# MLP input of a two-layer graph kernel: attention's output stored as two 16-bit planes, transposed by the DMA and joined on ScalarE

## The chip, the cores and the metric

The kernel runs on one core of one Trainium2 chip. The metric is the device time of one execution in microseconds (us). Three runs of the kernel before took 2292.01 us in the median (2291.98 to 2293.26).

## The reference, cut to what matters

3327 nodes with 1024 features pass through two layers, each added to its input. Layer 0 multiplies a dense adjacency matrix by a quantised product. Layer 1 is a graph attention with 8 heads of width 64, followed by an MLP of four dense layers:

```python
Wh = jnp.einsum('nf,hfd->hnd', x, W)
e = jax.nn.leaky_relu(e_src[:, :, None] + e_dst[:, None, :], ALPHA)
e = jnp.where(adj[None] > 0, e, NEG)
att = jax.nn.softmax(e, axis=-1)
h = jax.nn.elu(jnp.einsum('hnm,hmd->hnd', att, Wh))
enc = jnp.transpose(h, (1, 0, 2)).reshape(x.shape[0], -1)   # 3327 x 512
out = jax.nn.relu(enc @ W1.T + b1)     # 512 -> 256
out = jax.nn.relu(out @ W2.T + b2)     # 256 -> 256
out = jax.nn.relu(out @ W3.T + b3)     # 256 -> 512
out = out @ W4.T + b4                  # 512 -> 1024, added to x
```

All values are float32. The change concerns the way of `enc` from attention into the first of these dense layers.

## The kernel before, in words

The nodes are cut into 26 tiles of 128 rows. Layer 0 and the head projections fill the first part of the span. Attention runs as 32 passes (list `attends`), each for one head and one of four sets of 6 or 7 node tiles. A pass walks over 26 source tiles `j`. VectorE builds the selection `sel` (L729), TensorE multiplies it into up to seven accumulators (L738), and between these the generator `all_edges` feeds TensorE with a second product (L539), whose operand `mf` ScalarE casts from the mask (L538) and whose result `part` ScalarE copies out of PSUM (L543).

At the end of a pass ScalarE copies the accumulators to `xs` (L753), and the generator `close` finishes the pass a few instructions at a time while the next pass runs: VectorE sums and a reciprocal (L580 to L590), scaling on ScalarE (L593), the two activations of the ELU (L595, L596), the last step of the ELU on VectorE (L600), and one DMA from GpSimd's queue (L604), which stores a 64-column strip of 6 or 7 tiles into the DRAM tensor `enc_d`, 26 x 128 rows of 512 float32.

The MLP works on groups of four tiles (512 columns), seven groups with the last of two tiles. `load_nodes` (L664) loads a group's rows of `enc_d` (L667) and of the residual `x1_d` (L669) from SyncE's queue into one of two buffers, `nodes0` and `nodes1`, each of which holds an `enc` part and an `x1` part. The dense layers need features on partitions, so TensorE transposes `enc` in blocks of 128x128 against an identity matrix into PSUM (L797, name `tp`), ScalarE copies the four resulting blocks into `enct` (L800), and the function `dense` (L766) does a layer: matmuls (L772) and a ReLU with bias on ScalarE (L779). The last layer is kept with nodes on partitions (L809). VectorE adds the bias to `x1` (L805), then adds the product (L819), and SyncE's queue stores the result (L821). The first group's transposes and first dense layer are done during the last attention pass by the generator `first_layer` (L681: transposes L686, copies L691, matmuls L696, ReLU L704); its input sits in `nodes0`, and its `enct0` and `h1_0` in the tile `rest`.

The order of each engine's instructions is fixed before the run. A scheduler replays the program with estimated durations and puts each instruction into its engine's queue when its inputs and buffers are ready; earlier lines of the program go first where two are ready. On the chip each queue is then worked off in that order, and an instruction whose inputs are late holds up all behind it. Calls of `pin` fix VectorE's order in attention to the order of the program. Nothing in the MLP is pinned.

Buffers: `s3` holds the tiles of `close` (`ht3` with two buffers, the others one); the pool `s4` of the MLP has two buffers of each of `enct`, `h1`, `h2`, `h3`, `yo`; PSUM has four banks for `ps`/`tp4` and two double banks for the last product `o`.

Of the kernel before, what the change touches and what calls it, by code (L numbers as in the profile page):

```python
# [8 lines left out]
F32 = mybir.dt.float32  # L9
BF16 = mybir.dt.bfloat16  # L10
F32R = mybir.dt.float32r
U8 = mybir.dt.uint8
I8 = mybir.dt.int8
AF = mybir.ActivationFunctionType
ALU = mybir.AluOpType
# [4 lines left out]
P = 128  # L20
N = 3327
T = (N + P - 1) // P
NP = T * P
# [5 lines left out]
HD = 64  # L29
EMB = NH * HD  # L30
# [29 lines left out]
def two_layer_kernel(  # L60
# [23 lines left out]
    nc = tc.nc  # L84
# [15 lines left out]
    feat_d = dram.tile([T, NH, P, HW], F32, name="feat_d")  # L100
    dsum_d = dram.tile([T, NPAIR, P, HW], F32, name="dsum_d")
    src_d = [dram.tile([NH, len(sub) * P], F32, name=f"src_d{i}") for i, sub in enumerate(SUBS)]
    enc_d = dram.tile([NP, EMB], F32, name="enc_d")

    const.tile([P, 120], F32, name="gap")
    ndst = const.tile([P, T, NH], F32, name="ndst")
# [47 lines left out]
    def normaliser(mv, n, eps, factor, tag):  # L154

        rs = inverse_std(mv[:, :, 1], n, eps, tag)
        nc.vector.tensor_scalar(rs, rs, factor, None, ALU.mult)
        nb = small.tile([P, n], F32, tag=f"{tag}n", name=f"{tag}n")
        nc.vector.scalar_tensor_tensor(nb, mv[:, :, 0], -1.0, rs, ALU.mult, ALU.mult)
        return rs, nb  # L160

# [322 lines left out]
    with tc.tile_pool(name="f1", bufs=1, reuse_waits="tile") as f1p, tc.tile_pool(  # L486
# [81 lines left out]
        def close(i):  # L568


            c, g, e, si = attends[i]
            h = 2 * g + e
            sub = halves[c][si]
            nb = len(sub)
            md = mds[i // 4][:, sub[0] - 13 * c : sub[0] - 13 * c + nb, e * HC : (e + 1) * HC]
            sums = EDGE * (i // 4) + (EDGE if si else 7 * T)
            yield 0
            su = s3.tile([P, 7, 2, HC], F32, tag="su", name="su")
            s2d = su.rearrange("p b q c -> p b (q c)")
            pin(nc.vector.tensor_tensor(s2d[:, :nb], xs[:, :nb, 0], xs[:, :nb, 1], ALU.add))  # L580
            up, dn = su[:, :nb, 0], su[:, :nb, 1]
            for b, t in enumerate(sub):
                nc.scalar.activation(up[:, b], up[:, b], AF.Copy, scale=ratio[:, t, h : h + 1])  # L583
            yield sums
            pin(nc.vector.tensor_tensor(dn, md, dn, ALU.subtract))
            yield 0
            pin(nc.vector.tensor_tensor(up, up, dn, ALU.add))
            yield 0
            rs = small.tile([P, 7, 1], F32, tag="rs", name="rs")
            pin(nc.vector.reciprocal(rs[:, :nb], up[:, :, HD:]))  # L590
            ht = s3.tile([P, 7, HD], F32, tag="ht3", name="ht3", bufs=2)
            for b in range(nb):
                nc.scalar.activation(ht[:, b], up[:, b, :HD], AF.Copy, scale=rs[:, b])  # L593
            ex = s3.tile([P, 7, HD], F32, tag="ex", name="ex")
            nc.scalar.activation(ex[:, :nb], ht[:, :nb], AF.Relu, scale=-1.0)  # L595
            nc.scalar.activation(ex[:, :nb], ex[:, :nb], AF.Exp, scale=-1.0)  # L596
            yield 0

            pin(
                nc.vector.scalar_tensor_tensor(  # L600
                    ht[:, :nb], ex[:, :nb], -1.0, ht[:, :nb], ALU.add, ALU.max
                )
            )
            nc.gpsimd.dma_start(  # L604
                enc_d[sub[0] * P : (sub[-1] + 1) * P, h * HD : (h + 1) * HD].rearrange(
                    "(b p) d -> p b d", p=P
                ),
                ht[:, :nb],
            )

        def pin(ins):
            tc.keep_in_program_order(ins)
# [21 lines left out]
        for i, (c, g, e, si) in enumerate(attends):  # L634
            if i == len(attends) - 1:

                early.close()
                mlp = ctx.enter_context(ExitStack())

                def nodes(name):  # L640
                    n = large(mlp, name, [P, T * HW])
                    return (
                        n[:, : 4 * EMB].rearrange("p (q e) -> p q e", q=4),
                        n[:, 4 * EMB : 4 * (EMB + F)].rearrange("p (q e) -> p q e", q=4),
                    )

                weights = large(mlp, "weights", [P, T * HW])
                enc_x1 = [nodes("nodes0")]
                rest = large(mlp, "rest", [P, 7 * NP // 4])
                bb4 = rest[:, :F]  # L650
                bb1, bb2, bb3 = (rest[:, F + 4 * q : F + 4 * q + 4] for q in range(3))
                h1_0 = rest[:, F + 16 : F + 16 + D1 // P * 512].rearrange("p (m c) -> p m c", c=512)
                enct0 = rest[:, 2 * F + 16 : 2 * F + 16 + EMB // P * 512].rearrange(
                    "p (k c) -> p k c", c=512
                )
                w_at = iter((0, EMB * D1 // P, (EMB * D1 + D1 * D2) // P, (EMB * D1 + D1 * D2 + D2 * D3) // P))

                def weight(ap, k, m):
                    at = next(w_at)
                    wt = weights[:, at : at + k * m].rearrange("p (k m) -> p k m", k=k)  # L660
                    nc.sync.dma_start(wt, ap.rearrange("(k p) m -> p k m", p=P))
                    return wt

                def load_nodes(i, t0):  # L664
                    enc, x1 = enc_x1[i]
                    for q, t in enumerate(range(t0, min(t0 + 4, T))):
                        nc.sync.dma_start(enc[:, q, :], enc_d[t * P : (t + 1) * P, :])  # L667
                    for q, t in enumerate(range(t0, min(t0 + 4, T))):
                        nc.sync.dma_start(x1[:, q, :], x1_d[t * P : (t + 1) * P, :])  # L669

                load_nodes(0, 0)
                w1 = weight(w1t, EMB // P, D1)
                with nc.allow_non_contiguous_dma(reason="biases of a few hundred elements"):
                    for bb, ap in ((bb1, b1), (bb2, b2), (bb3, b3)):
                        m = ap.shape[0] // P
                        nc.sync.dma_start(bb[:, :m], ap.rearrange("(m p) -> p m", p=P))
                w2, w3 = weight(w2t, D1 // P, D2), weight(w3t, D2 // P, D3)
                w4 = weight(w4t, D3 // P, F)
                nc.sync.dma_start(bb4, b4.partition_broadcast(P))

                def first_layer():  # L681

                    for k in range(EMB // P):
                        tp = m_ps.tile([P, 512], F32, tag="mps", name="tp0")
                        for q in range(4):
                            nc.tensor.transpose(  # L686
                                tp[:, q * P : (q + 1) * P],
                                enc_x1[0][0][:, q, k * P : (k + 1) * P],
                                ident,
                            )  # L690
                        nc.scalar.copy(enct0[:, k], tp)  # L691
                        yield
                    for m in range(D1 // P):
                        ps = m_ps.tile([P, 512], F32, tag="mps", name="h0_ps")
                        for k in range(EMB // P):
                            nc.tensor.matmul(  # L696
                                ps,
                                w1[:, k, m * P : (m + 1) * P],
                                enct0[:, k],
                                start=(k == 0),  # L700
                                stop=(k == EMB // P - 1),
                            )
                            if k == EMB // P - 1:
                                nc.scalar.activation(  # L704
                                    h1_0[:, m], ps, AF.Relu, bias=bb1[:, m : m + 1]
                                )
                            yield

                first_group = first_layer()
            h = 2 * g + e  # L710
# [49 lines left out]
    with tc.tile_pool(name="s4", bufs=2, reuse_waits="tile") as s4, tc.tile_pool(  # L760
# [23 lines left out]
        for g, t0 in enumerate(range(0, T, 4)):  # L784
            tiles = range(t0, min(t0 + 4, T))
            cols = len(tiles) * P
            enc, x1 = enc_x1[g % 2]
            if t0 + 4 < T:
                load_nodes((g + 1) % 2, t0 + 4)
            if g == 0:  # L790
                h1 = h1_0
            else:
                enct = s4.tile([P, EMB // P, 512], F32, name="enct")
                for k in range(EMB // P):
                    tp = ps_p.tile([P, 512], F32, tag="ps", name="tp4")
                    for q, t in enumerate(tiles):
                        nc.tensor.transpose(  # L797
                            tp[:, q * P : (q + 1) * P], enc[:, q, k * P : (k + 1) * P], ident
                        )
                    nc.scalar.copy(enct[:, k, :cols], tp[:, :cols])  # L800
                h1 = dense(enct, EMB // P, w1, bb1, D1 // P, cols, "h1")
            h2 = dense(h1, D1 // P, w2, bb2, D2 // P, cols, "h2")
            h3 = dense(h2, D2 // P, w3, bb3, D3 // P, cols, "h3")
# [61 lines left out]
```

## Time and profile before

| | |
|---|---|
| median of 3 runs | 2292.01 us |
| the profiled execution | 2293.44 us |
| its span, first to last instruction | 2291.7 us |
| TensorE busy | 2233.5 us, 97% |
| VectorE busy | 1559.1 us, 68% |
| ScalarE busy | 998.2 us, 44% |
| GpSimd busy | 119.3 us, 5% |
| mean granted TensorE clock | 0.995 |
| MLP after attention's last matmul | about 1989.8 to 2287 us of the span |

A matmul's record can overlap that of its neighbours, so a busy TensorE is read from what it gets through in a stretch rather than from its share. In the rows, "idle before" is the time that the engine stood idle just ahead of these instructions, followed by what ended it. Weight loads of TensorE have rows of their own (PEld). SPq and POOLq rows are DMA issues of SyncE and GpSimd.

### The profile page before, as it was taken

Reading aid. Unit: us, or ns where it says so; the run is one execution under the profiler, and the core shown is the slowest. Engines: PE = TensorE matmul, PEld = TensorE weight load, DVE = VectorE, ACT = ScalarE, POOL = GpSimd, SP = SyncE. Lnnn points to the kernel's source line nnn. Section 1 sums busy time; section 2 is a strip of 40 time slices with the busy share of each in tenths; the row PEclk is TensorE's granted clock in tenths of the full one; section 3 lists DMA queues with packets and bytes.
Section 4 is the critical chain, followed back from the end, with each engine's and each line's share of the span. In section 5 each row is a group of like instructions: output and inputs, shape, how many; then the busy total and the mean of one; then the engine's idle time right before and its main releaser. Section 6 shows DMA issues by size and latency. Waiting matters only on the chain. (4 is left out here: it accounts for less than half of the span.)

```text
span 2291.7 us, 32041 instructions
## 1 busy us (share of the span) xinstructions
PE 2233.5 (97%) x12896; PEld 1785.0 (78%) x12896; DVE 1559.1 (68%) x2090; ACT 998.2 (44%) x1654; POOL 119.3 (5%) x173
## 2 busy tenths in 40 slices
PE   4999999999999999889999999999999999999999
PEld 2467777777777777579999999999999999744444
DVE  7845555555555555487999999999999999732211
ACT  4753333333333333346555555555555555411120
POOL 0000110111101111000000000000000000000000
PEclk9999999999999999999999999999999999999999
DMA  6324444444445444763324142654242422343311
GB/s 234 129 82 149 151 150 142 162 145 155 151 141 162 151 149 152 239 210 118 99 73 134 45 142 80 215 178 154 84 144 77 141 87 75 112 152 123 125 55 55
DMA packets 150301, 304.94 MB, mean 133 GB/s; under 512 B 10172, under 2 KB 91020, under 8 KB 150152
## 3 DMA queue, kind: packets, MB, share of 16 engines
q1 hardware_dynamic: 130248, 229.72, 30.3%
q0 software_dynamic: 19904, 73.17, 9.9%
q8 instruction: 101, 1.65, 0.3%
q14 instruction: 48, 0.39, 0.1%
HBM read 216.07 MB, written 86.79 MB: 132 GB/s over the span
## 5 line engine op out<-in xcount | busy, mean ns | idle before, releaser
L729 DVE SCALAR_TENSOR_TENSOR sel<-srow,ndst,mask 128x896 fp32r<-128x896 f32 (+1 forms) x832 | 864.1, 1079 | 54.4 <-PE acc L738 41.2
L539 PE MATMUL mps<-dw,mf 128*128 128x260 f32 x2704 | 453.3, 283 | 0.1
L444 PE MATMUL mm<-s_int,hi 128*128 128x512 f32 x1352 | 433.0, 399 | 0.0
L444 PE MATMUL mm<-s_int,lo 128*128 128x512 f32 x1352 | 421.6, 391 | 0.0
L738 PE MATMUL acc<-f_even,sel 128*128 128x260 f32 x2704 | 396.9, 284 | 1.4 <-DVE sel L729 1.1
L738 PE MATMUL acc<-f_odd,sel 128*128 128x260 f32 x2704 | 395.0, 286 | 0.0
L538 ACT CAST mf<-mask 128x1664 fp32r<-128x1664 uint8 x208 | 331.3, 1593 | 123.5 <-PE mps L539 100.2
L539 PEld LDWEIGHTS mps<-dw,mf 128*128 128x128 f32 x2704 | 377.7, 188 | 0.3 <-ACT part L543 0.3
L738 PEld LDWEIGHTS acc<-f_odd,sel 128*128 128x128 f32 x2704 | 353.4, 188 | 7.3 <-issue 3.1
L738 PEld LDWEIGHTS acc<-f_even,sel 128*128 128x128 f32 x2704 | 354.9, 188 | 5.4 <-DVE sel L729 2.8
L444 PEld LDWEIGHTS mm<-s_int,lo 128*128 128x128 f32 x1352 | 253.8, 188 | 57.6 <-issue 5.7
L444 PEld LDWEIGHTS mm<-s_int,hi 128*128 128x128 f32 x1352 | 252.1, 188 | 55.6 <-issue 5.7
L184 DVE TENSOR_SCALAR mk<-at 128x896 uint8<-128x896 f32 x104 | 61.7, 594 | 267.1 <-DMA at<-in_adj_t 266.1
L179 ACT CAST hi<-at 128x896 fp32r<-128x896 f32 x104 | 92.7, 891 | 328.8 <-PE mm L444 294.8
L385 PE MATMUL whm<-whead,ht 128*128 128x512 f32 x416 | 186.7, 602 | 0.8 <-ACT ht L382 0.8
L809 PE MATMUL o<-weights,h 128*128 128x512 f32 x416 | 179.7, 592 | 0.0
L809 PEld LDWEIGHTS o<-weights,h 128*128 128x128 f32 x416 | 79.0, 190 | 99.1 <-issue 99.0
L385 PEld LDWEIGHTS whm<-whead,ht 128*128 128x128 f32 x416 | 77.4, 191 | 98.0 <-issue 87.8
L183 DVE TENSOR_TENSOR lo<-at,hi 128x896 fp32r<-128x896 f32 x104 | 106.6, 1025 | 49.0 <-ACT hi L179 38.8
L543 ACT COPY part<-mps 128x260 f32<-128x260 f32 x104 | 39.3, 378 | 223.9 <-PE mps L539 223.9
L819 DVE TENSOR_TENSOR yo<-o,nodes 128x1024 f32<-128x1024 f32 (+1 forms) x27 | 31.8, 1182 | 139.2 <-PE o L809 139.2
L333 PE MATMUL mm<-w_int,xqt 128*128 128x512 bf16 x416 | 97.7, 386 | 10.2 <-DVE w_int L319 7.7
(136 smaller groups left out, 1567.8 us busy)
## 6 DMA issues: line engine op xcount, KB each, us to landing
feat_d<-fw POOLq DMA_DIRECT2D x26, 1040.0 KB, 5.3
f_even<-feat_d SPq DMA_DIRECT2D x7, 3380.0 KB, 13.1
f_odd<-feat_d SPq DMA_DIRECT2D x7, 3380.0 KB, 12.3
at<-in_adj_t SPq DMA_DIRECT2D x52, 448.0 KB, 4.2
at<-in_adj_t SPq DMA_DIRECT2D x52, 384.0 KB, 3.2
mask<-mask_d SPq DMA_DIRECT2D x39, 416.0 KB, 6.9
dw<-dsum_d SPq DMA_DIRECT2D x16, 910.0 KB, 8.9
dsum_d<-dw POOLq DMA_DIRECT2D x26, 520.0 KB, 6.5
```

The source lines that it names most:

```text
L179: ins = nc.scalar.copy(hi, at)
L183: nc.vector.tensor_tensor(lo, at, hi.bitcast(F32), ALU.subtract)
L184: nc.vector.tensor_scalar(mk[:, r], at, 0.0, None, ALU.is_gt)
L333: nc.tensor.matmul(mm[:, c * 512 : (c + 1) * 512], xqts[t][:, k, :], w_int[:, k, c * 512 : (c + 1) * 512], start=(k == 0), stop=(k == KF - 1),
L385: nc.tensor.matmul(whm, ht[:, k, :], whead[:, k, :], start=(k == 0), stop=(k == KF - 1))
L444: nc.tensor.matmul(mm[:, c * 512 : (c + 1) * 512], which[:, q, :], s_int[j][:, c * 512 : (c + 1) * 512], start=(j == 0 and which is hi), s ...
L538: nc.scalar.copy(mf, mask[:, j : j + TH, :])
L539: nc.tensor.matmul(ps, mf[:, j % TH, :], dw[:, j, :], start=(j == 0), stop=(j == T - 1))
L543: nc.scalar.copy(part[:, i % 7], ps.rearrange("p (q c) -> p q c", q=2))
L729: nc.vector.scalar_tensor_tensor(sel[:, :nb], srow[:, :nb], ndst[:, j, h : h + 1], mask[:, :, j, :], ALU.is_gt, ALU.mult,)
L738: nc.tensor.matmul(accs[b], sel[:, b, :], f[:, j, :], start=(j == 0), stop=(j == T - 1))
L809: nc.tensor.matmul(ps[:, c * 512 : (c + 1) * 512], h3[:, k, q * P : (q + 1) * P], w4[:, k, c * 512 : (c + 1) * 512], start=(k == 0), stop= ...
```

## The change

`enc_d` becomes a tensor of two planes of 16-bit integers: the low and the high halves of each float32. At the end of `close` a ScalarE copy (tile `eh`, one buffer) splits the words of `ht` into the two halves, and GpSimd issues two DMAs, one for each plane, in place of one. `load_nodes` reads a group's rows with two transposing DMAs (one for each plane, issued from SyncE's queue) in place of up to four plain ones; features then lie on partitions. A ScalarE copy for each of the four blocks of 128 features interleaves the two halves again into float32. TensorE's transposes and the copies out of PSUM are gone. For the first group the joining copies take the place of the transposes in `first_layer`; for the others they are written in the program one group ahead, right after the loads of the next group.

```diff
-    enc_d = dram.tile([NP, EMB], F32, name="enc_d")
+    enc_d = dram.tile([2, NP, EMB], U16, name="enc_d")
...
+    def halves_of_words(words):
+
+        return words.bitcast(U16).rearrange("p (n two) -> p two n", two=2)
...
-            nc.gpsimd.dma_start(
-                enc_d[sub[0] * P : (sub[-1] + 1) * P, h * HD : (h + 1) * HD].rearrange(
-                    "(b p) d -> p b d", p=P
-                ),
-                ht[:, :nb],
-            )
+            eh = s3.tile([P, 2, 7 * HD], U16, tag="eh", name="eh")[:, :, : nb * HD]
+            nc.scalar.copy(eh, halves_of_words(ht[:, :nb].rearrange("p b d -> p (b d)")))
+            for q in range(2):
+                nc.gpsimd.dma_start(
+                    enc_d[q, sub[0] * P : (sub[-1] + 1) * P, h * HD : (h + 1) * HD].rearrange(
+                        "(b p) d -> p b d", p=P
+                    ),
+                    eh[:, q].rearrange("p (b d) -> p b d", d=HD),
+                )
...
-                        n[:, : 4 * EMB].rearrange("p (q e) -> p q e", q=4),
+                        n[:, : 4 * EMB].bitcast(U16).rearrange("p (q r) -> p q r", q=2),
...
+                def by_feature(enc, cols):
+
+                    k = EMB // P
+                    return enc[:, :, : k * cols].rearrange("p q (k c) -> p q k c", k=k)
+
                 def load_nodes(i, t0):
                     enc, x1 = enc_x1[i]
-                    for q, t in enumerate(range(t0, min(t0 + 4, T))):
-                        nc.sync.dma_start(enc[:, q, :], enc_d[t * P : (t + 1) * P, :])
+                    rows = slice(t0 * P, min(t0 + 4, T) * P)
+                    for q in range(2):
+                        nc.sync.dma_start_transpose(by_feature(enc, rows.stop - rows.start)[:, q], enc_d[q, rows])
...
                     for k in range(EMB // P):
-                        tp = m_ps.tile([P, 512], F32, tag="mps", name="tp0")
-                        for q in range(4):
-                            nc.tensor.transpose(
-                                tp[:, q * P : (q + 1) * P],
-                                enc_x1[0][0][:, q, k * P : (k + 1) * P],
-                                ident,
-                            )
-                        nc.scalar.copy(enct0[:, k], tp)
+                        nc.scalar.copy(
+                            halves_of_words(enct0[:, k]), by_feature(enc_x1[0][0], 512)[:, :, k]
+                        )
                         yield
...
-            enc, x1 = enc_x1[g % 2]
+            x1 = enc_x1[g % 2][1]
+            enct = following if g else None
             if t0 + 4 < T:
                 load_nodes((g + 1) % 2, t0 + 4)
+                following = s4.tile([P, EMB // P, 512], F32, name="enct")
+                n = (min(t0 + 8, T) - t0 - 4) * P
+                for k in range(EMB // P):
+                    nc.scalar.copy(
+                        halves_of_words(following[:, k, :n]),
+                        by_feature(enc_x1[(g + 1) % 2][0], n)[:, :, k],
+                    )
             if g == 0:
                 h1 = h1_0
             else:
-                enct = s4.tile([P, EMB // P, 512], F32, name="enct")
-                for k in range(EMB // P):
-                    tp = ps_p.tile([P, 512], F32, tag="ps", name="tp4")
-                    for q, t in enumerate(tiles):
-                        nc.tensor.transpose(
-                            tp[:, q * P : (q + 1) * P], enc[:, q, k * P : (k + 1) * P], ident
-                        )
-                    nc.scalar.copy(enct[:, k, :cols], tp[:, :cols])
                 h1 = dense(enct, EMB // P, w1, bb1, D1 // P, cols, "h1")
```

More of the change, by code (lines that the diff above doesn't have):

```diff
@@ L12 @@
 U8 = mybir.dt.uint8
+U16 = mybir.dt.uint16
 I8 = mybir.dt.int8
```

## The prediction

> **What bounds the kernel now.** I read the page's busy times first, then the chain that ended last in order of time, because the change is in one stage. From 1992 us on, the chain is nearly all TensorE. One full group of four tiles:
>
> ```profile
> PE 2233.5 (97%) x12896; PEld 1785.0 (78%) x12896; DVE 1559.1 (68%) x2090; ACT 998.2 (44%) x1654; POOL 119.3 (5%) x173
> ...
> 2028.68 1.75 PE tp L797 x16
> 2030.42 17.54 PE h_ps L772 x40
> 2047.97 27.47 PE o L809 x64
> 2075.43 1.75 PE tp L797 x16
> ...
> 2262.46 0.87 PE tp L797 x8
> ```
>
> A group is 1.75 + 17.54 + 27.47 = 46.76 us of TensorE, end to end, and nothing stands between. So what the transposes take in this chain is really on the path: five full groups (1 to 5) and the half group 6.
>
> Next, the groups by shape from 1960 us on, the copies that the change removes, and, from the whole span, the one ScalarE copy of as many 16-bit elements as the new ones:
>
> ```profile
> L797 PE MATMUL tp<-ident,nodes 128*128 128x128 f32 x88 | 10.6, 273 | 0.0
> L800 ACT COPY enct<-tp 128x512 f32<-128x512 f32 x20 | 10.3, 600 | 136.2 <-PE tp L797 136.2
> ...
> L284 ACT COPY xqt<-tp 128x1024 bf16<-128x1024 bf16 x26 | 26.1, 1005 | 2.0 <-PE tp L282 1.9
> ```
>
> ScalarE idles 136 us here waiting for TensorE, so it has room. Where this room lies I read from its timeline in group 1:
>
> ```profile
> 2037.33 0.69 ACT L779 ACTIVATE h<-h_ps,rest 128x512 f32<-128x512 f32 x1 [2.75 <-PE h_ps L772]
> 2039.23 0.69 ACT L779 ACTIVATE h<-h_ps,rest 128x512 f32<-128x512 f32 x1 [1.22 <-PE h_ps L772]
> 2040.95 0.69 ACT L779 ACTIVATE h<-h_ps,rest 128x512 f32<-128x512 f32 x1 [1.03 <-PE h_ps L772]
> ```
>
> After the last ReLU of a group, at 2048.7 us, it does nothing until 2075.9. SyncE's queue shows when loads go out:
>
> ```profile
> 1969.47 1.78 SPq L667 DMA_DIRECT2D nodes<-enc_d  x4
> ...
> 2001.41 1.75 SPq L667 DMA_DIRECT2D nodes<-enc_d  x4
> 2003.20 2.03 SPq L669 DMA_DIRECT2D nodes<-x_d  x4
> 2011.26 0.34 SPq L821 DMA_DIRECT2D out<-yo  x1
> ...
> 2031.49 2.00 SPq L667 DMA_DIRECT2D nodes<-enc_d  x3
> 2056.12 0.34 SPq L821 DMA_DIRECT2D out<-yo  x1
> ```
>
> The loads at 1969.47 are those of group 2: they go out as soon as `nodes0` has been read (SyncE waited 8.9 us for the transposes L686), some 105 us before group 2 begins. The scheduler thus hoists loads about two groups ahead.
>
> **What the Trainium skill says.** "Advanced Engine Details and Errata", X-Bar Transpose (TRN2): transposing DMAs are as fast as regular ones, 350 to 400 GB/s expected. "DMA: Bandwidth & Descriptors", Latency and other measured facts: 261 GB/s on one kernel. "VectorE: DVE Perf Modes", The three transpose paths: 1309 ns for one 128x128 bf16 block. The trace before has no transposing DMA, so none of these is confirmed. "ScalarE: Activation LUTs", What ACT_TABLE_LOAD costs: an ACTIVATE with immediate operands takes 186 ns + 0.833 ns an element, which is 1039 ns for 1024; the trace agrees (1005 ns, row L284).
>
> **The change part by part.**
>
> *Removed from the MLP:* 5 x 1.75 + 0.87 = 9.6 us of TensorE on the path. The 24 copies L800 (11.5 us) go too, but ScalarE wasn't the bound.
>
> *Removed from the last pass of attention:* 16 transposes, about 16 x 0.109 = 1.75 us of TensorE. VectorE is busy 48.8 of the 50 us from 1940 to 1990 and paces this pass (TensorE's weight loads wait for `sel` at 1963, 1966 and 1970 us), so a lighter TensorE mostly waits longer. Between 0 and 1.75 us; I take 0.
>
> *Transposing DMAs:* 14 in place of 26 loads, two for each group, 1.05 MB a pair. At 261 to 400 GB/s a pair is 2.6 to 4 us of transfer (an estimate from the two pages), at 32 blocks x 1309 ns it is 42 us. The nearest row, four plain loads of 256 KB, lands about 4 us after its last issue. I take 5 to 10 us to landing, since the pieces are short. The cover: a buffer's `enc` part is free once the joining copies of the group in it are done, about 13 us into the group before last, and is wanted a whole group later. On the queue the pair stands behind the last `x1` load (2030.97) and ahead of the next store (2056.12). From 13 us into the group that leaves some 13 us free, and the two banks of `o` and two buffers of `yo` forgive about 6 us more: with a tile each 6.87 us and L819 at 1.22 us, VectorE may be 5.6 us late. Cost 0 up to some 19 us a pair; what lies above is paid in each group.
>
> *Joining copies:* 28 in place of 28 copies, but of 1024 16-bit elements: 1.0 us each for 0.6, 4.0 us a group. They may start when the `enct` buffer of the group before last is free, after a group's last h1 matmul (2037.3), so likely between the ReLUs above, in gaps of 1.22 and 1.03 us, or after them in 27 us of idle time. One ReLU is sensitive, the last of h2 (2040.95), since the second half of h3's first product waits for it: at most 0.1 us late with a copy of 1.0 us, 1 us with one twice as long. I take 0.1 us x 5 groups = 0.5 us; bounds 0 and 5.
>
> *Change of stage (1989 to 2015 us):* ScalarE is busy 8.1 of 11 us from 1990 on, and TensorE already waits for two ReLUs (0.57 and some 1.5 us). The copies of group 2 can fall here, as its loads are in long before: four copies of 1 us in a queue with 3 us of room. I take 1 us; bounds 0 and 4. Group 1's loads wait for the last store of attention. That store now follows a ScalarE copy (0.8 us) and a second issue (0.9 us), so the pair goes out near 2004.3 instead of 2001.4, and the `x1` loads queue behind it. VectorE stood idle 10.8 us for the first of these (until 2008.87), with L819 of the first tile behind it in its queue. TensorE needs this bank back at 2014.8. A delay of 3 + 4 us puts L819's end at 2018 unless the new order has it ahead of that L805. I take 1 us; bounds 0 and 6.
>
> *Splitting copies:* 16 of 896 and 16 of 768 elements. The casts of as many float32 elements (L179) take 945 and 837 ns, so 16 x 0.945 + 16 x 0.837 = 28.5 us of ScalarE over some 930 us of attention. Each waits for VectorE (L600); behind it on ScalarE stand the mask casts `mf` and the copies `part`, for which TensorE waits. The cover is the idle time of ScalarE:
>
> ```profile
> L538 ACT CAST mf<-mask 128x1664 fp32r<-128x1664 uint8 x208 | 331.3, 1593 | 123.5 <-PE mps L539 100.2 <-issue 21.6 <-ACT su L583 1.1
> L593 ACT ACTIVATE ht<-su,rs 128x64 f32<-128x64 f32 x208 | 53.5, 337 | 66.7 <-DVE rs L590 36.2 <-issue 30.0 <-ACT h L779 0.3
> L543 ACT COPY part<-mps 128x260 f32<-128x260 f32 x104 | 39.3, 378 | 223.9 <-PE mps L539 223.9
> L539 PE MATMUL mps<-dw,mf 128*128 128x260 f32 x2704 | 453.3, 283 | 0.1
> ```
>
> ScalarE already stands at L593 for VectorE, 66.7 us in all, and TensorE's L539 lost 0.1 us. One more such wait has the 223.9 us ahead of `part` to lie in. I take 0.5 us; bounds 0 and 28.5, all uncovered. The 32 added issues of GpSimd are 32 x 0.91 = 29 us on an engine that is 5% busy, and hidden. The stores' pieces shrink from 256 to 128 bytes at unchanged bytes, while the DMA is about a third busy in attention: hidden.
>
> *Sum:* -9.6 + 0.5 + 1 + 1 + 0.5 = -6.6 us. Against the profiled execution (2293.44, of which 2291.7 are span) that is 2286.8; that execution was 1.4 us above the median, so on the median's footing 2292.0 - 6.6 = 2285.4.
>
> **The rivals.**
>
> *A wash (chance 0.2).* The savings stand, but the change of stage and attention take 5 to 10 us: the bounds of 4 and 6 us both met, or a fifth of the splitting copies uncovered. For it: `mps` has one PSUM bank, so a late `part` stops L539 at once. Against: no stall of L539 before. 2292.0 - 9.6 + 10 = 2292.4, range 2287.5 to 2296.5.
>
> *Slow crossbar (0.17), the one on the other side.* The pair takes longer than the 19 us that the queue forgives, and stores, `x1` loads and the joining copies are late in each group. It decides from 19 us a pair. At 25 us: 5 groups x 6 us - 9.6 = +20, 2312; at 42 us: 5 x 23 - 9.6 = +105, 2397. For it: the 1309 ns. Against: the two bandwidths, which put the pair at 4 us.
>
> *Order on ScalarE (0.15).* The copies of the next group stand in ScalarE's queue ahead of the ReLUs of the current one, and these wait for the transposes or for four copies in a row: 4 us less the 1 to 2 us of slack in a group, or more where a transfer is late. From 1.75 us a group it eats the gain. At 3 us over 6 groups: +18 - 9.6 = +8, 2300. For it: the copies come first in the program. Against: loads two groups ahead.
>
> **How the numbers follow.** The forecast (2281 to 2287.5 as its own range: 1.75 us of attention's transposes gained and no losses, against twice the losses) has 0.48. 0.2% is 4.6 us, about what a measurement here can tell from no change. Faster 0.48; within 0.2%, the wash, 0.2; slower 0.32, from the last two. From the forecast's low end of 2281 up to 2310 the range leaves out most of the slow crossbar and little else, about 0.18.
>
> **What would show it.** Right: a chain of h_ps and o alone, 45.0 us a group; no TensorE transposes from 1960 us on; transposing DMAs landing within 10 us; joining copies near 1.0 us whose idle time ends on TensorE or DMA without a ReLU behind. L539's idle time stays below 1 us. Wrong: waits of L819 or L805 for DMA, of h_ps for ReLUs over 1 us a group, or a later end of attention than 1989 us. My weakest number is the crossbar's time, for which no row stands.

## The result, and the profile after

The changed kernel takes 2282.07 us in the median (2281.76 to 2283.57, 4 runs) against 2292.11 us of four runs of the kernel before, timed beside it: -10.0 us, ratio 0.9956 with a 95% interval of 0.9939 to 0.9974. The time lies inside the predicted range, below the predicted 2285.4; the direction was as forecast, the size was 10.0 where 6.6 was said. The profiled execution has a span of 2281.8 us against 2291.7, 9.9 us less, so the two profiles can be set against each other.

The chain that ended last, of the kernel after (its longer pieces: start in us, length in us, what): a group of the MLP with joining copies among its ReLUs, the first of three such, and then one without.

```profile
2000.07 27.47 PE o L818 x64
2027.54 6.88 PE h_ps L781 x16
2035.03 2.53 ACT enct L803 x2
2038.15 7.19 PE h_ps L781 x16
2045.34 27.47 PE o L818 x64
...
2163.31 17.56 PE h_ps L781 x40
2180.87 27.47 PE o L818 x64
```

The 1.75 us of transposes ahead of each group are gone. Groups 1, 2 and 3 take 45.27, 45.25 and 45.25 us (from 2027.54 to 2072.81, 2118.06 and 2163.31), groups 4 and 5 take 45.02 and 45.01; all took 46.76 before. In the first three, two joining copies have come into the chain, which was TensorE's alone.

The groups of instructions of the kernel after, over the whole span (busy time, mean ns of one, idle time before and its cause): TensorE's second product of attention, the copy behind it, and the new splitting copies.

```profile
L544 PE MATMUL mps<-dw,mf 128*128 128x260 f32 x2704 | 453.6, 283 | 0.1
L548 ACT COPY part<-mps 128x260 f32<-128x260 f32 x104 | 39.2, 377 | 194.4 <-PE mps L544 194.4
L610 ACT COPY eh<-ht 128x896 uint16<-128x896 uint16 (+1 forms) x32 | 28.3, 884 | 7.0 <-DVE ht L605 7.0
```

The same view by shape, from 1945 us on:

```profile
L803 ACT COPY enct<-nodes 128x1024 uint16<-128x1024 uint16 x20 | 25.3, 1333 | 9.4 <-DMA nodes<-enc_d 9.4
```

The 28.3 us of splitting copies stand in the shadow of `part`: its idle time went from 223.9 to 194.4 us, and TensorE's L544 lost the same 0.1 us as before. The joining copies take 1333 ns, not the 1.0 us of the prediction.

SyncE's queue of the kernel after: the transposing DMAs, of group 0, group 2, group 1 and then group 3.

```profile
1927.91 4.98 SPq L681 DMA_TRANSPOSE nodes<-enc_d  x2
1963.40 11.53 SPq L681 DMA_TRANSPOSE nodes<-enc_d  x2
2003.31 4.74 SPq L681 DMA_TRANSPOSE nodes<-enc_d  x2
2008.11 2.00 SPq L683 DMA_DIRECT2D nodes<-x_d  x4
2015.14 4.93 SPq L681 DMA_TRANSPOSE nodes<-enc_d  x1
```

A pair occupies SyncE for about 5 us, since each issue takes about 2.5 us; a single one lands 5.0 us after its issue (median). The pair at 1963.40 took 11.5 us, while the weights of the MLP were being loaded. The loads are hoisted as before, group 2's even ahead of group 1's.

Stage by stage, from the starts in the two traces: up to the loads of group 0 the kernel after is 0.36 us earlier (1927.91 for 1928.27), although the splitting copies and their stores came on top; across the kernels below this mark lies between 1926.8 and 1929.5, so 0.36 us can't be told from their spread. From there to h2's first matmul of group 0 it takes 60.75 us (to 1988.66) where 61.53 (to 1989.80) were needed: -0.78. From there to the first matmul after group 0 both take 38.88 us: 0. From there to the end 254.26 us for 263.02: -8.76. Together -9.9 us.

### The profile page after: what moved, and what is told of

It reads as the page before. It is cut to its first block, busy times and chain, and to the rows that moved or that the text cites. A ratio compares the mean times of both kernels' runs of the same rounds, so it can differ in the third digit from the quotient of the medians.

```text
span 2281.8 us, 31860 instructions
## 1 busy us (share of the span) xinstructions
PE 2222.5 (97%) x12780; PEld 1774.4 (78%) x12792; DVE 1559.8 (68%) x2090; ACT 1040.8 (46%) x1686; POOL 147.7 (6%) x205
## 4 chain that ended last, share of the span: by engine, by line
PE 52%; ACT 1%; DVE 0%; DMA 0%; issue 0%; SPq 0%; DVEq 0%
PE acc L747 27%; PE mps L544 13%; PE o L818 8%; PE h_ps L781 4%; ACT enct L803 0%; PE h_ps L705 0%; DMA weights<-in_w1t 0%; DVE sel L738 0%; ACT h L788 0%; DVE nodes L814 0%; ACT su L588 0%; SPq L690 0%; DVE su L585 0%; DVE yo L828 0%; DVEq L871 0%
## 5 line engine op out<-in xcount | busy, mean ns | idle before, releaser
L544 PE MATMUL mps<-dw,mf 128*128 128x260 f32 x2704 | 453.6, 283 | 0.1
L544 PEld LDWEIGHTS mps<-dw,mf 128*128 128x128 f32 x2704 | 378.0, 188 | 0.4 <-ACT part L548 0.3
L548 ACT COPY part<-mps 128x260 f32<-128x260 f32 x104 | 39.2, 377 | 194.4 <-PE mps L544 194.4
L828 DVE TENSOR_TENSOR yo<-o,nodes 128x1024 f32<-128x1024 f32 (+1 forms) x27 | 31.9, 1183 | 138.1 <-PE o L818 137.9
L788 ACT ACTIVATE h<-h_ps,rest 128x512 f32<-128x512 f32 (+1 forms) x54 | 35.1, 653 | 196.1 <-PE h_ps L781 196.1
```

What stands on the lines that cost most here:

```text
L544: nc.tensor.matmul(ps, mf[:, j % TH, :], dw[:, j, :], start=(j == 0), stop=(j == T - 1))
L548: nc.scalar.copy(part[:, i % 7], ps.rearrange("p (q c) -> p q c", q=2))
```

## The experiments

The kernel before ran 2294.56 us (16 runs) beside the first four of these and 2293.26 us (23 runs) beside the last four, a little slower than with the result above, so medians are compared through the ratio to it, and single steps by the traces.

**Only the added work of attention.** The kernel before, with the split and the plane stores added to it:

```diff
+            eh = s3.tile([P, 2, 7 * HD], U16, tag="eh", name="eh")[:, :, : nb * HD]
+            words = ht[:, :nb].rearrange("p b d -> p (b d)").bitcast(U16)
+            nc.scalar.copy(eh, words.rearrange("p (n two) -> p two n", two=2))
+            for q in range(2):
+                nc.gpsimd.dma_start(
+                    planes_d[q, sub[0] * P : (sub[-1] + 1) * P, h * HD : (h + 1) * HD].rearrange(
+                        "(b p) d -> p b d", p=P
+                    ),
+                    eh[:, q].rearrange("p (b d) -> p b d", d=HD),
+                )
```

> The kernel before, with the splitting copy and the two plane stores added to each close; the planes are never read, the float32 store and TensorE's transposes stay. If the split lies wholly in ScalarE's idle time, as priced (0.5 us), the time stays at 2292 us within 1.5 us, attention's last matmul ends within 1 us of where it ended before, and L539's product has no new idle time. If the ScalarE time of 28.5 us is uncovered, it ends near 2320; a fifth uncovered gives 2298.

Measured: 2294.08 us, ratio 1.0001 (0.9993 to 1.001). From group 0's loads to h2's first matmul it takes 61.50 us (1929.00 to 1990.50), as before. The split costs nothing that can be measured (the interval is 2 us wide to each side), and the uncovered ends (2298 and 2320) are out.

**Twice the split.** The changed kernel, with the copy written twice:

```diff
             nc.scalar.copy(eh, halves_of_words(ht[:, :nb].rearrange("p b d -> p (b d)")))
+            nc.scalar.copy(eh, halves_of_words(ht[:, :nb].rearrange("p b d -> p (b d)")))
```

> The changed kernel with each splitting copy done twice into the same tile: another 28.5 us of ScalarE in attention, and stores that start 0.9 us later. If ScalarE's idle time covers it, 2282 to 2284 us, and what is lost stands at the change of stage only. If the first copy had used up the cover, up to 2310.

Measured: 2284.49 us, ratio 0.996 (0.9945 to 0.9975), as the changed kernel. The groups of the whole span show where the second copy went:

```profile
L544 PE MATMUL mps<-dw,mf 128*128 128x260 f32 x2704 | 452.7, 283 | 0.1
L548 ACT COPY part<-mps 128x260 f32<-128x260 f32 x104 | 39.3, 377 | 177.9 <-PE mps L544 177.5
```

Another 16.5 us of idle time ahead of `part` are used up, L544 still waits 0.1 us, and the last pass takes 60.63 us (1928.58 to 1989.21). The cover was good for at least 57 us of copies. The change of stage behind it takes 39.20 us (to 2028.41) for 38.88: some 0.3 us are lost there, as expected, and the chain that ended last now runs through the last split's store, the transposing DMAs and an `x1` load.

**The first group by TensorE.** The changed kernel, with tiles 0 to 3 also stored as float32 and transposed in the last pass the old way:

```diff
+            if sub[0] == 0:
+                nc.gpsimd.dma_start(
+                    enc_f[:, h * HD : (h + 1) * HD].rearrange("(b p) d -> p b d", p=P), ht[:, :nb]
+                )
...
-                        nc.scalar.copy(
-                            halves_of_words(enct0[:, k]), by_feature(enc_x1[0][0], 512)[:, :, k]
-                        )
+                        tp = m_ps.tile([P, 512], F32, tag="mps", name="tp0")
+                        for q in range(4):
+                            nc.tensor.transpose(
+                                tp[:, q * P : (q + 1) * P],
+                                words(enc_x1[0][0])[:, q, k * P : (k + 1) * P],
+                                ident,
+                            )
+                        nc.scalar.copy(enct0[:, k], tp)
```

> The changed kernel, but tiles 0 to 3 go the old way: float32 strips of the first seven tiles are stored as well (8 added stores), loaded plainly, and transposed by TensorE in the last attention pass. If VectorE paces that pass, as the prediction's step said (gain 0), the time stays at 2282. If the 16 transposes were on the path there, attention's last matmul ends 1 to 1.8 us later and the time is 2283 to 2284.

Measured: 2285.32 us, ratio 0.9961 (0.9947 to 0.9975), too close to tell by time. By the trace the last pass is back at 61.52 us (1929.44 to 1990.96), as before the change (61.53), where the changed kernel needs 60.75. The 16 transposes, with the plain loads ahead of them, cost this pass 0.77 us, somewhat under the 1 us that the expectation gave them. Neither 0 nor all of their 1.75 us; why not all is taken up under the last pass below.

**Joining copies behind the last ReLU.** The changed kernel, with the copies written after h3 in the program and pinned there:

```diff
-                for k in range(EMB // P):
-                    nc.scalar.copy(
-                        halves_of_words(following[:, k, :n]),
-                        by_feature(enc_x1[(g + 1) % 2][0], n)[:, :, k],
-                    )
...
             h3 = dense(h2, D2 // P, w3, bb3, D3 // P, cols, "h3")
+            if t0 + 4 < T:
...
+                for k in range(EMB // P):
+                    ins = nc.scalar.copy(
+                        halves_of_words(following[:, k, :n]),
+                        by_feature(enc_x1[(g + 1) % 2][0], n)[:, :, k],
+                    )
+                    tc.keep_in_program_order(ins)
```

> The changed kernel with the joining copies queued behind the last ReLU of each group, where ScalarE has nothing to do for 27 us. In the changed kernel groups 1 to 3 take 45.27, 45.25 and 45.25 us where groups 4 and 5, which have no full joining copies among their ReLUs, take 45.02 and 45.01. If the copies among the ReLUs cost this 0.25 us a group, all five groups take 45.0 us and the end is 0.75 us earlier (2281.3). If the difference has another cause, nothing moves. A loss of over 1 us a group would mean that a copy is late for the next group's first matmul.

Measured: 2283.36 us, ratio 0.9953 (0.9938 to 0.9968). Its chain that ended last:

```profile
2045.98 27.47 PE o L820 x64
2073.45 17.54 PE h_ps L781 x40
2090.99 27.47 PE o L820 x64
2118.45 17.54 PE h_ps L781 x40
```

All five groups take 45.0 us, so the quarter of a microsecond came from the copies' place among the ReLUs. From the first matmul of `o` to the end it is 0.53 us shorter than the changed kernel (281.20 for 281.73): three groups gain 0.25 each, and group 0 loses 0.17. By the trace this is the better order; by time the two kernels can't be told apart.

**Twice and four times the transposing DMAs.** The changed kernel, with `n` = 2 and 4:

```diff
-                    for q in range(2):
+                    for q in list(range(2)) * n:
                         nc.sync.dma_start_transpose(by_feature(enc, rows.stop - rows.start)[:, q], enc_d[q, rows])
```

> The changed kernel with each pair of transposing DMAs issued twice into the same place, so that the crossbar has twice the work in each group. If a pair costs nothing below some 19 us, as the prediction's slow rival put it, two pairs (some 10 to 18 us of issue and transfer) still lie in the free stretch of the queue: 2282 to 2284 us, groups of 45.0 to 45.3 us, with at most a few us lost at the change of stage, where stores stand behind them. If the queue has no room to spare, each group is longer by what a pair takes, 5 to 9 us: 2310 to 2335.

Measured: 2293.02 us, ratio 1.0 (0.9992 to 1.0009). Neither expectation held: groups 2 and later keep 45.3 or 45.0 us, and yet the gain is gone. It is lost in one place. ScalarE and then TensorE in group 1, from the timeline of two pairs a group:

```profile
2035.61 0.69 ACT L788 ACTIVATE h<-h_ps,rest 128x512 f32<-128x512 f32 x1 [1.22 <-PE h_ps L781]
2043.29 2.51 ACT L803 COPY enct<-nodes 128x1024 uint16<-128x1024 uint16 x2 [7.00 <-DMA nodes<-enc_d]
2045.68 0.67 ACT L788 ACTIVATE h<-h_ps,rest 128x512 f32<-128x512 f32 x1
...
2046.40 7.03 PE L781 MATMUL h_ps<-h,weights 128*128 128x512 f32 x12 [7.40 <-ACT h L788]
```

The joining copies of group 3 stand between the ReLUs of h2 in group 1. Group 3's transposes can start only once `nodes1` has been read for group 1, so they are the latest of all; here the last of them went out at 2035.82 and ScalarE stood still for 7.0 us, with a ReLU behind it for which TensorE waited 7.4 us. Group 1 takes 54.1 us for 45.27, which is 1.4 us more than the wait explains: the 12 matmuls behind the wait take 7.03 us, where the 12 ahead of it took 5.50, and the profile gives a granted TensorE clock of 0.76 from 2046.4 to 2053.2 us, against 1.00 from 2053.4 on. The spans differ by 7.8 us (2289.6 and 2281.8).

> The same with four times: some 20 to 36 us of transposing DMAs a group, over the stated point of 19 us. By the slow rival's price the excess is paid in each of five groups: 5 x (1 to 17) us, 2287 to 2367, and TensorE waits in the last product for VectorE, which waits for x1 loads or stores behind the transposes. If what matters is only that all is landed within a group of 45 us, the time stays at 2282 to 2287.

Measured: 2310.14 us, ratio 1.0068 (1.0051 to 1.0084). The issues on SyncE's queue, from the timeline of four pairs a group:

```profile
2004.74 19.22 SPq L681 DMA_TRANSPOSE nodes<-enc_d  x8
```

The waits from 1990 us on (total us, times, longest):

```profile
PE o L818 <- DVE yo L828: 18.5, 2, 9.6
```

The piece of the chain behind the first of these two waits:

```profile
2076.77 9.84 PE o L818 x16
```

VectorE's timeline:

```profile
2074.35 1.23 DVE L814 TENSOR_TENSOR nodes<-nodes,rest 128x1024 f32<-128x1024 f32 x1 [18.96 <-DMA nodes<-x_d]
```

Eight of 512 KB take 19.2 us back to back, 2.4 us each or 218 GB/s. Now the mechanism of the slow rival is there too: an `x1` load stands behind the transposes, VectorE waits 19 us for it with the sum L828 behind, and TensorE waits for its bank. But this happens twice (18.5 us in all), not in five groups: loads run ahead, so the last transposes of the kernel start at 2130, and groups 4 and 5 take 45.0 us again. The slow matmuls are there as well: 16 of `o` take 9.84 and 9.61 us behind the two waits, where a quarter of the usual 27.47 us is 6.87, at granted clocks of 0.72 (2076.8 to 2086.5 us) and 0.74 (2135.3 to 2144.7). So 5.7 us more are lost in the same two groups, which take 12.3 and 13.0 us longer than in the changed kernel.

**Four joining copies in a row.** The changed kernel, with the copies of the next group pinned between h1 and h2, and h2's ReLUs pinned behind them (the last argument of `dense` pins each ReLU):

```diff
+            if t0 + 4 < T:
...
+                for k in range(EMB // P):
+                    ins = nc.scalar.copy(
+                        halves_of_words(following[:, k, :n]),
+                        by_feature(enc_x1[(g + 1) % 2][0], n)[:, :, k],
+                    )
+                    tc.keep_in_program_order(ins)
-            h2 = dense(h1, D1 // P, w2, bb2, D2 // P, cols, "h2")
+            h2 = dense(h1, D1 // P, w2, bb2, D2 // P, cols, "h2", g > 0)
```

> The changed kernel with the four joining copies of the next group put in a row behind the ReLUs of h1 and ahead of the two ReLUs of h2, in groups 0 to 5. This is the order that the rival on ScalarE's order described. Four copies take 5.1 us; the ReLUs of h2 wait for them, and h3 waits for these. By the rival's price (3 us a group) 2282 + 5 x 3 = 2297; worked out from the changed kernel's trace, the second ReLU of h2, due 3.5 us after h1's last matmul, comes after 0.7 + 5.1 + 0.7 = 6.5 us, so 2.5 to 3 us a group in groups 1 to 4 and less in group 5, whose copies are half as long: 2293 to 2297. If order on ScalarE is of no matter, 2282.

Measured: 2294.19 us, ratio 1.0004 (0.9996 to 1.0013). Its chain:

```profile
2074.90 6.88 PE h_ps L781 x16
...
2087.87 7.13 PE h_ps L781 x16
2095.01 27.47 PE o L822 x64
```

A group takes 47.57 us (2047.44 to 2095.01), 2.56 us more than without copies among the ReLUs, as worked out from the trace; TensorE waits 2.48 us for the ReLU behind the four copies. No operation was added to the changed kernel; its order alone takes back the whole gain.

**Joining copies that don't interleave.** The changed kernel, with the low halves left out and the words of groups 1 to 6 made of high halves side by side:

```diff
-                        halves_of_words(following[:, k, :n]),
-                        by_feature(enc_x1[(g + 1) % 2][0], n)[:, :, k],
+                        following[:, k, :n].bitcast(U16).rearrange("p (two n) -> p two n", two=2),
+                        by_feature(enc_x1[(g + 1) % 2][0], n)[:, 1:2, k].to_broadcast([P, 2, n]),
```

> The changed kernel, with the joining copies of groups 1 to 6 written as two runs side by side and both read from the plane of high halves, so that the low halves are left out and the halves aren't interleaved; the number and size of the copies stay. In the changed kernel a copy of 1024 elements takes 1333 ns where 1005 was expected. If writing every other 16-bit word costs the third, a copy here takes about 1.0 us and groups 1 to 3 take 45.0 to 45.1 us. If the 16-bit integer type or reading from SBUF costs it, a copy stays at 1.33 us and the groups at 45.25.

Measured: 2281.52 us, ratio 0.9947 (0.9931 to 0.9964). By shape, from 2000 us on:

```profile
L803 ACT COPY enct<-nodes 128x1024 uint16<-128x1024 uint16 x20 | 19.9, 1040 | 9.6 <-DMA nodes<-enc_d 9.6
```

1040 ns for the same number of elements of the same type from the same place: so the 0.29 us on top come with the interleaved write, every other 16-bit word. (The source is also one plane twice instead of two planes; no run separates the two.) Groups 1 to 3 take 44.82 us, even a little less than groups without any copies (45.01). TensorE's queue is in another order there: between the weight loads that wait for h2's two ReLUs stand four matmuls, where the groups without copies have two, so that TensorE waits less for the second ReLU (its weight loads idle for 0.26 us ahead of it, at 2037.73, against 0.75 us at 2039.70 in the kernel with the copies behind the last ReLU). Groups 1 to 3 of the changed kernel have the same order as here. So their 0.25 us is a net sum: about 0.44 us (45.26 less 44.82) for the copies of 1333 ns, less 0.19 for the order.

## Why the prediction was right, and where it was off

*What bounds the MLP.* Right. The chain is TensorE's, and what its transposes took is gone: 8.76 us of the 9.6 from the end of group 0 on; of the difference, 0.75 is the joining copies' part in groups 1 to 3.

*Last pass of attention.* The step took 0 because VectorE paces this pass. It was 0.78 us, and the old transposes put back make the pass as long as before. The step misread two things. TensorE was as busy as VectorE, 48.72 us of the 50 (the first busy time in this row of the kernel before, followed by weight loads and VectorE):

```profile
1940.00:1990.00 50.00, 48.72 (x355) 43.71 (x354) 48.79 (x54) 17.48 (x46) 1.81 (x2) 1.00 0.33 109
```

And the waits for `sel` that it names were waits of weight loads, 0.15 to 0.21 us each; TensorE's matmuls never waited for `sel` in this pass. So TensorE's load counted. That only 0.78 of 1.75 us came out goes with a new wait of the changed kernel, in which the first dense layer starts before its weights have landed:

```profile
1964.69 1.12 PE L705 MATMUL h_ps<-rest,weights 128*128 128x512 f32 x2 [0.97 <-DMA weights<-in_w1t]
```

In the seven kernels whose last pass has no transposes this wait is 0.52 to 0.97 us, and the pass is longer by as much, 60.29 to 60.75 us. Less the wait, 59.75 to 59.80 us are left in each, an estimate of the pass with the weights in time: about 1.75 us below the 61.50 to 61.53 us with transposes. No run loads these weights earlier, so this part is not shown.

*Transposing DMAs.* The size was right: the pair sent at 2003.31 was read from 2010.19 on, 6.9 us later and within "5 to 10", and it was hidden in all groups. The point from which it would decide was wrong. The step looked at stores and `x1` loads behind the pair and put this point at 19 us a pair, paid in each group. With twice the DMAs, 9.4 us of issues a group, the gain is gone already, by another way: a joining copy in ScalarE's queue that waits for the transposes of group 3, with ReLUs behind it. The rival on ScalarE's order named this wait; the step on the DMAs left it out. And the excess is paid in the one or two groups in which loads cannot run ahead, not in five. Of the Trainium skill's figures, the 350 to 400 GB/s of "Advanced Engine Details and Errata", X-Bar Transpose (TRN2), and the 261 GB/s of "DMA: Bandwidth & Descriptors", Latency and other measured facts, were nearer than the estimate of 42 us from the 1309 ns a block of "VectorE: DVE Perf Modes", The three transpose paths; but the runs show 218 GB/s, below both.

*Joining copies.* The term was mis-sized: 1333 ns each where 1.0 us was taken from a copy with a contiguous destination. It cost 0.25 us net in three groups, 0.75 us where 0.5 was said, since the gaps between the ReLUs take most of it.

*Change of stage.* 2 us were taken for it, 0 measured: 38.88 us before and after. The copies of group 2 did not fall among the ReLUs there; they ran behind group 1's, eight copies in a row from 2010.19 on. The `x1` loads went out 4.9 us later, less than the 7 us of the step, whose 0.8 + 0.9 us for the later store also make 2003.1 and not 2004.3 (measured 2003.31). What kept TensorE from waiting is that the new order has the first tile's sum (L828, at 2006.97) ahead of the addition that waits for them, the exception that the step allowed for. This is most of the forecast's error.

*Splitting copies.* 0.5 us were taken, and no cost is found, alone on the kernel before or doubled on the one after: TensorE's product ahead of `part` lost 0.1 us in each. The reading of the 223.9 us ahead of `part` was right.

So of the 3.3 us between the forecast of -6.6 and the -9.9 of the spans, 2 are the change of stage, 0.8 the last pass, 0.5 the split and 0.4 the shift ahead of the change, less the 0.3 by which the MLP gained less than its -9.1 (figures rounded). The forecast's own upper end of 2287.5 is a slip: twice the losses of 3.0 us give 2288.4. The wash and the slow side didn't come, but the wash lay near: twice the transposes, or the same copies in another order, give the time of the kernel before.

## What to carry to other kernels

Where one engine's chain is closed, the time of what leaves it is the gain, and the work that replaces it costs by its place in the queues more than by its length: 28 us of copies in idle time cost nothing here, doubled as well, while four copies ahead of a ReLU cost 2.6 us a group. When a load is hoisted, look for the one buffer whose turn comes last; the instruction that waits for that load, and what stands behind it, decide how slow the load may be. A wait of TensorE's can cost more than its length: behind those of 7.4 to 9.6 us the matmuls ran slower for a while. And two engines can both be near 100% busy in a stretch: then see whose instructions wait for the other before calling one of them free. A copy that nothing waits for soon belongs where its engine is idle anyway, not ahead of work that is waited for.

## What the runs showed of the hardware

- The issue of a transposing DMA of 512 rows by 512 16-bit elements keeps SyncE's queue for 2.4 us when they come back to back (eight in 19.2 us, 218 GB/s), where the plain loads of 256 KB before took 0.4 us of issue. It lands 5.0 us after its issue (median). One issue, at 1963.4 us, took 8.5 us while the weights of the MLP (512 KB to 2 MB each) were moving.
- ScalarE copies 1024 16-bit elements in 1040 ns to contiguous places and in 1333 ns to every other 16-bit word. Reading every other word adds nothing that shows: the splitting copy of 768 elements takes 832 ns, against an estimate from the Trainium skill's "ScalarE: Activation LUTs", What ACT_TABLE_LOAD costs, of 186 + 0.833 x 768 = 826 ns.
- Behind waits of TensorE of 7.4, 8.9 and 9.6 us in the MLP the granted clock was 0.76, 0.72 and 0.74 over the next 7 to 10 us, and 16 matmuls of `o` took 9.84 and 9.61 us for 6.87. Behind four waits of 2.48 us (four joining copies in a row) it was 1.00.
